# VectorE's two-operand operations read one operand from PSUM, and norms are finished in pairs, in a four-layer graph network on one core

## The chip, the cores and the metric

The kernel runs on one core of one Trainium2 chip. The metric is the device time of the whole program in microseconds (us), the median of three runs. Everything is computed in fp32.

## The reference

Input are 128 graphs of 128 nodes with 512 features each, `x` of 128x128x512, and their adjacency matrices `adj` of 128x128x128, and the weights of four layers. Each layer adds a graph function to `x` and normalises the sum over the features. Cut to what matters here, per graph:

```python
# layer 0: a diffusion with attention weights, three hops
Xw = x @ Wv + bv;  sj, si = Xw @ aw[:512], Xw @ aw[512:]
alpha = adj * exp(leaky_relu(sj[None, :] + si[:, None] + ab, 0.2))
T = alpha / (alpha.sum(-1, keepdims=True) + 1e-12)
H = sum over k in 0..2 of (T^k @ x) @ Wk[k] + bk[k]
x1 = layernorm(x + relu(H))
# layer 1: two hypergraph convolutions, H = (adj != 0)
conv(v, W, b) = Dn * (H @ (Be * (H.T @ (v @ W.T)))) + b
h = layernorm(relu(conv(x1, W1, b1))) * gamma + beta       # 1024 features
x2 = layernorm(x1 + (conv(h, W2, b2) + x1))
# layer 2: s = (x2 @ w) @ a
A = exp(leaky(tanh((s[:, None] + s[None, :]) / 8) * 8, 0.1)) * adj
A = A / A.sum(-1, keepdims=True) * adj.sum(-1, keepdims=True)
x3 = layernorm(x2 + A @ x2 @ w)
# layer 3: attention of 8 heads, scores scaled by 2 * adj, softmax, output product
out = layernorm(x3 + softmax(q k^T / 8 * 2 * adj) v Wo^T + bo)
```

## The kernel before

**Tiling.** One graph is one block of 128 rows. A pair of graphs (`U` = 2) is one tile; a round of `layer0`, `layer1` or `layer23` works on two pairs, so there are 32 rounds of four graphs for each. All of layer 0 is done, then all of layer 1, then layers 2 and 3 together; results pass through DRAM (`x1d`, `x2d`, `x3d`). The large products are split by Strassen's scheme in Winograd's form, seven products of half-size blocks in place of eight (`strassen`, L614), for some weights twice over (`twice`, L817). TensorE gathers into three PSUM banks per scheme; ScalarE copies the first results of a bank out (`plain_take`, L659), VectorE adds the later ones to tiles in SBUF (`biased_take`, L674), and GpSimd makes the sums of the left operands (`lefts`, `operands`).

**The order of the work.** No engine's order is written by hand. Every operation is handed to a planner (`Plan`, L171) with a key (a due time in rounds), and the planner plays all of them through with estimated durations (`estimate`, L122) and hand-off times (`LATENCY`): on each engine it takes the lowest key among those that are ready, gives out buffers as they come free, and at last issues everything in the order of its start times (`emit`, L362). So nearly all instructions have line 373 in the profile, and groups are told apart by tiles. A change of any estimate, tile or dependency can reorder every queue. Engines then run their queues strictly in that order. DMAs are issued on SyncE's queue (SP), save a few at the start.

**What the planner knows of VectorE and GpSimd.** `shares_port` (L148) marks operations that it keeps apart on these two engines: all of GpSimd's but memsets, and of VectorE those with two SBUF operands and one-operand copies and scalar operations from SBUF. In `order` a marked operation starts after the end of the other engine's last marked one (`port`, L284 and L331).

**Buffers.** PSUM has eight banks of 128x512: six named `bank`, and `t0` and `t1`, which layer 0 uses for its hops and which join the banks when layer 0 is over. In SBUF, `four` are tiles of a pair (128x2x512), `sq` pairs of 128x128 matrices, `col` small statistics, `out`, `first`, `side`, `ks` and `rows` large areas that are cut into further `four` tiles when their first use is over. A trace name such as `out<-bank,out` therefore often means a `four` tile that lies in the `out` area.

**The steps that the change touches.**
- Attention terms of layer 0 (L1000 and before) and layer 2 (`layer23`): PE spreads a column over a bank (`spread_pair`, L834); ScalarE applies the nonlinear functions from the bank into an `sq` tile and then within it; VectorE multiplies it by the adjacency matrix, both in SBUF, and sums the rows (`accum_out`); GpSimd divides by the sums, and the matrix goes through DRAM to be turned.
- Counts of layer 1: VectorE takes the maximum of two-column counts with 1.
- Row scale of layer 1: for each graph, VectorE computes `h * dn + b1` over 128x1024 in one operation (`t`, `rows1`), ScalarE applies relu, VectorE takes statistics.
- Norms: `norm_terms` (L690) and `layer_norm` (L701) finish each 128-row block by itself: VectorE sums up the statistics and adds eps, GpSimd raises the variance to the power -1/2, ScalarE multiplies by the mean, ScalarE applies both to the block.
- Closing sum of layer 1: per graph `bw2 * drd + b2` and `2 * x1 + q`, ahead of the last product, then `p * dn + q` from the bank, all on VectorE.
- Layer 3's softmax (`attention`, L1421): the weights go through DRAM to be turned by VectorE, except in the very last pair (`last`), where PE transposes them.

Of the kernel before, what the change touches and what calls it, by code (L numbers as in the profile page):

```python
# [66 lines left out]
SPARE, AHEAD = 4, 6  # L67
SIZE = {"four": U * D, "sq": U * (P + 2), "bank": D, "col": 12, "row": D, "w28": 7168, "q7": 7 * 2 * P,
# [102 lines left out]
class Plan:  # L171
# [64 lines left out]
    def order(self, urgent=None):  # L236
# [71 lines left out]
        while count < n:  # L308
# [21 lines left out]
            if o[6]:  # L330
                port[DVE + POOL - e] = end  # L331
                stale.add(DVE + POOL - e)
# [49 lines left out]
def kernel(  # L382
# [80 lines left out]
    def col(*n):  # L463
        return tile_of("col", *n)
# [225 lines left out]
    def norm_terms(st, n=1):  # L690
        mv = col(2)
        ve.bn_aggr(mv, st[:, :6 * n])
        ve.tensor_scalar(mv[:, 1:2], mv[:, 1:2], EPS, None, op0=OP.add)
        ve.tensor_scalar(mv[:, 0:1], mv[:, 0:1], -1.0, None, op0=OP.mult)
        rstd = col(1)
        po.tensor_tensor(rstd, mv[:, 1:2], neghalf, OP.pow)
        nmr = col(1)
        ac.mul(nmr, mv[:, 0:1], rstd)
        return nmr, rstd

    def layer_norm(t):  # L701

        st = col(12)
        stats(st, 0, t)
        nmr, rstd = norm_terms(st)
        ac.activation(t, t, AF.Identity, bias=nmr, scale=rstd)

    def normed(take, t):

        def then(f, b):  # L710
            def run(p):
                f(p)
                layer_norm(t[:, b])
            return run
        take["c12"] = then(take["c12"], 0)
        take["c21"] = then(take["c21"], 1)
        return take
# [232 lines left out]
    def layer0(i0):  # L950
# [33 lines left out]
        for r, i in enumerate(both):  # L984
            A = load_adj(i)
            plan.key = base + WHENT[0][r]
            s = col(U)
            ac.activation(s, R[r][:, :, 0, 3 * P + 1], AF.Identity, bias=c0)
            pt = spread_pair([R[r][:, b, 0, 3 * P:3 * P + 1].to_broadcast([P, P]) for b in range(U)])
            e = sq()  # L990
            for b in range(U):
                ac.activation(e[:, b], pt[:, b * P:(b + 1) * P], AF.Prelu, bias=s[:, b:b + 1], alpha=0.2)
            ac.activation(e, e, AF.Exp)
            den = col(U)
            for b in range(U):
                ve.scalar_tensor_tensor(e[:, b], e[:, b], 1.0, A[:, b], op0=OP.mult, op1=OP.mult,
                                        accum_out=den[:, b:b + 1])
            ac.activation(den, den, AF.Identity, bias=tiny)
            ve.reciprocal(den, den)
            for b in range(U):  # L1000
                po.tensor_scalar(e[:, b], e[:, b], den[:, b:b + 1], None, op0=OP.mult)
            loads.append(through_dram(e.rearrange("p b (k w) -> p b k w", w=Q), f"e{i}"))
        for r, i in enumerate(both):
            plan.key = base + WHENT[1][r]
            x0 = load_rows(x[i:i + U].rearrange("b p f -> p b f"))
            TT = pair_turned(loads[r])
            for m in (1, 0):
                for b in range(U):
# [5 lines left out]
                    if m:  # L1014
                        ac.copy(to, by)
                    else:
                        ve.scalar_tensor_tensor(x0[:, b], p, 0.0, x0[:, b], op0=OP.max, op1=OP.add)
                        layer_norm(x0[:, b])
# [116 lines left out]
    def layer1(i0):  # L1135
# [5 lines left out]
        for (_, ab), in each(loaded):  # L1141
# [7 lines left out]
            ve.tensor_scalar(cnt, cnt, 1.0, None, op0=OP.max)  # L1149
# [52 lines left out]
        for r, i in enumerate(both):  # L1202
            plan.key = base + STEP1 * (5, 7)[r]
            for b in range(U):
                t = h[r][b].rearrange("p g f -> p (g f)")
                ve.scalar_tensor_tensor(t, t, dns[r][b], rows1[:, :2].rearrange("p g f -> p (g f)"),
                                        op0=OP.mult, op1=OP.add)
                ac.activation(t, t, AF.Relu)
                sts = col(12)
                for g in range(2):  # L1210
                    stats(sts, g, h[r][b][:, g])
                nmr, rstd = norm_terms(sts, 2)
                ac.activation(t, t, AF.Identity, bias=nmr, scale=rstd)
                loads.append(through_dram(h[r][b].rearrange("p (j g) (k w) -> p j (g k) w", j=1, k=2), f"h{i + b}"))
        for r, i in enumerate(both):
# [15 lines left out]
            q = four()  # L1231
            for b in range(U):
                ve.scalar_tensor_tensor(q[:, b], bw2, drds[r][:, b:b + 1], b2_b, op0=OP.mult, op1=OP.add)
                ve.scalar_tensor_tensor(q[:, b], x1[:, b], 2.0, q[:, b], op0=OP.mult, op1=OP.add)
            for b in range(U):
                p = bank()
                pe.matmul(p, K[:, b, :P], G[:, b], start=True, stop=True)
                ve.scalar_tensor_tensor(q[:, b], p, dns[r][b], q[:, b], op0=OP.mult, op1=OP.add)
                layer_norm(q[:, b])
            sp.dma_start(x2d[i // U], q)  # L1240
# [91 lines left out]
    def layer23(i0):  # L1332
# [10 lines left out]
        for i, x2, A in each(both, x2s, As):  # L1343
# [5 lines left out]
            pt = spread_pair([s2[:, b:b + 1].to_broadcast([P, P]) for b in range(U)])  # L1349
            F = sq()  # L1350
            for b in range(U):
                ac.activation(F[:, b], pt[:, b * P:(b + 1) * P], AF.Tanh, bias=s2[:, b:b + 1])
            ac.activation(F, F, AF.Prelu, alpha=0.1)
            ac.activation(F, F, AF.Exp, scale=8.0)
            r = col(U)
            for b in range(U):
                ve.scalar_tensor_tensor(F[:, b], F[:, b], 1.0, A[:, b], op0=OP.mult, op1=OP.mult,
# [63 lines left out]
    def attention(i0, A, qT, kT, v, x3d, base, r):  # L1421
        last = i0 + U == B
# [129 lines left out]
```

## Time and profile before

| | before |
|---|---|
| median of 3 runs (lowest, highest) | 5461.58 us (5458.56, 5464.62) |
| the profiled execution | 5463.22 us, span 5461.4 us |
| mean granted TensorE clock | 0.994 |
| instructions | 93,897 |
| VectorE, attention products sq<-sq,sq 128x128 | 256, 402 ns mean |
| VectorE, row scale 128x1024, in three areas | 63 + 47 + 18, 1619, 1584 and 1722 ns mean |
| VectorE, bank and SBUF, 128x512 (four<-bank,sq) | 72, 679 ns mean |
| GpSimd, powers col<-col,neghalf | 640, 582 ns mean |
| ScalarE, products col<-col,col | 640, 291 ns mean |
| DMA | 815.8 MB, 149 GB/s |

PE is TensorE's matmul row, PEld its weight loads, DVE is VectorE, ACT ScalarE, POOL GpSimd, SP SyncE; `x256` counts records, and an fp32 matmul shows as two. A group line reads: line, engine, operation, tiles written <- tiles read, shape, count, busy us, mean ns, and then the idle time ahead of it with what ended that.

### The profile page before, as it was taken

How to read it: one execution, taken by the hardware profiler on the slowest of the kernel's cores; microseconds unless marked ns; L12 is line 12 of the kernel's file. 1: busy time of each engine (PE TensorE's matmuls, PEld its weight loads, DVE VectorE, ACT ScalarE, POOL GpSimd, SP SyncE). 2: the span in 40 equal slices, each digit the busy share in tenths (PEclk: the TensorE clock that was granted, in tenths of full speed). 3: DMA queues.
4: the chain of work that ended last, by engine and by line, in shares of the span. 5: the costliest groups of instructions: out<-in, count | busy, mean ns of one | idle time of the engine just before them, and what ended most of it. 6: DMA issues, size and time to landing. Idle time of an engine off the chain costs nothing.

```text
span 5461.4 us, 93897 instructions
## 1 busy us (share of the span) xinstructions
PE 5338.6 (98%) x29065; PEld 4256.9 (78%) x29065; DVE 4544.2 (83%) x11573; ACT 2382.0 (44%) x6437; POOL 4032.8 (74%) x4875
## 2 busy tenths in 40 slices
PE   8999999999999999999999999999999999999998
PEld 4555555555778888888888888998999998999987
DVE  6889888887888989998989878787787887787776
ACT  2434433344434444444444344554444444545444
POOL 6777777665777777777777567877777777777776
PEclk9999999999999999999999999999999999999999
DMA  3444444445454554554545645555555555455443
GB/s 100 134 139 125 133 143 128 128 120 162 146 149 150 145 155 150 151 157 147 154 146 150 225 139 159 167 155 157 162 154 164 156 158 161 153 163 162 153 153 123
DMA packets 841933, 815.80 MB, mean 149 GB/s; under 512 B 269388, under 2 KB 640596, under 8 KB 841431
## 3 DMA queue, kind: packets, MB, share of 16 engines
q1 hardware_dynamic: 839926, 807.18, 48.7%
q8 instruction: 230, 3.77, 0.3%
q10 hardware_dynamic: 1504, 2.62, 0.2%
q14 instruction: 273, 2.23, 0.1%
HBM read 459.43 MB, written 350.09 MB: 148 GB/s over the span
## 4 chain that ended last, share of the span: by engine, by line
PE 76%; DVE 10%; DMA 4%; POOL 3%; SPq 3%; issue 2%; ACT 1%; DVEq 0%; POOLq 0%; ACTq 0%
PE bank L373 58%; PE t L373 19%; DVE out L373 3%; DVE four L373 3%; SPq L373 3%; DVE col L373 2%; POOL four L373 1%; DVE side L373 1%; DMA sq<-in_adj_dram 1%; POOL out L373 1%; DMA first<-x3d 1%; DMA four<-in_x_dram 0%; DMA out<-x3d 0%; ACT out L373 0%; DVE sq L373 0%
## 5 line engine op out<-in xcount | busy, mean ns | idle before, releaser
L373 PE MATMUL bank<-first,four 128*128 128x386 f32 (+3 forms) x6114 | 1733.2, 430 | 58.4 <-DVE out L373 21.8
L373 PEld LDWEIGHTS bank<-first,four 128*128 128x128 f32 (+2 forms) x6114 | 1070.3, 189 | 640.1 <-DVE out L373 132.1
L373 DVE TENSOR_TENSOR out<-bank,out 128x386 f32<-128x386 f32 (+1 forms) x2030 | 981.6, 502 | 211.9 <-PE bank L373 164.2
L373 POOL TENSOR_TENSOR col<-col,neghalf 128x1 f32<-128x1 f32 x640 | 368.7, 582 | 452.1 <-DVE col L373 451.5
L373 DVE TENSOR_TENSOR four<-bank,four 128x256 f32<-128x256 f32 x1256 | 514.8, 416 | 177.5 <-PE bank L373 158.3
L373 POOL TENSOR_TENSOR out<-out 128x772 f32<-128x772 f32 (+3 forms) x250 | 350.2, 1408 | 263.2 <-DVE out L373 189.4
L373 PE MATMUL bank<-first,out 128*128 128x256 f32 (+2 forms) x2048 | 498.7, 377 | 7.5 <-DVE side L373 2.8
L373 POOL TENSOR_TENSOR four<-four 128x256 f32<-128x256 f32 (+2 forms) x439 | 357.6, 827 | 142.7 <-DVE four L373 76.1
L373 ACT COPY out<-bank 128x258 f32<-128x258 f32 (+2 forms) x527 | 214.1, 409 | 550.7 <-PE bank L373 414.2
L373 PEld LDWEIGHTS bank<-first,out 128*128 128x128 f32 (+2 forms) x2048 | 372.3, 189 | 77.3 <-issue 9.5
L373 POOL TENSOR_TENSOR four<-four,four 128x256 f32<-128x256 f32 (+2 forms) x479 | 414.0, 869 | 7.2 <-PE bank L373 1.3
L373 ACT ACTIVATE col<-col,col 128x1 f32<-128x1 f32 x640 | 183.9, 291 | 401.0 <-POOL col L373 348.5
L373 PE MATMUL bank<-first 128*128 128x128 f32 (+1 forms) x2356 | 329.6, 278 | 1.9 <-DVE four L373 1.3
L373 ACT ACTIVATE four<-four,col,col 128x512 f32<-128x512 f32 (+1 forms) x367 | 324.2, 887 | 7.4
L373 PEld LDWEIGHTS bank<-first 128*128 128x128 f32 (+1 forms) x2356 | 300.5, 189 | 18.1 <-issue 2.9
L373 PE MATMUL bank<-out,first 128*128 128x128 f32 (+2 forms) x1832 | 301.0, 305 | 1.1 <-DVE col L373 0.8
L373 ACT COPY four<-bank 128x256 f32<-128x256 f32 (+1 forms) x329 | 137.7, 422 | 355.5 <-PE bank L373 333.5
L373 DVE BATCH_NORM_STATS2 col<-four 128x6 f32<-128x512 f32 x430 | 287.6, 678 | 4.8 <-ACT four L373 3.1
L373 PEld LDWEIGHTS bank<-out,first 128*128 128x128 f32 (+1 forms) x1832 | 250.1, 187 | 19.4 <-issue 1.5
L373 PE MATMUL t<-out,sq 128*128 128x512 f32 x512 | 255.5, 594 | 6.4 <-DVE sq L373 2.5
L373 PE MATMUL bank<-four,first 128*128 128x256 f32 (+3 forms) x1424 | 253.3, 322 | 2.7 <-DVE first L373 1.1
L373 ACT COPY t<-out 128x512 f32<-128x512 f32 x256 | 151.0, 591 | 198.6 <-DVE four L373 107.2
(567 smaller groups left out, 12925.7 us busy)
## 6 DMA issues: line engine op xcount, KB each, us to landing
four<-x1d SPq DMA_DIRECT2D x69, 512.0 KB, 5.2
four<-h SPq DMA_DIRECT2D x66, 512.0 KB, 4.5
four<-in_x_dram SPq DMA_DIRECT2D x504, 64.0 KB, 2.1
h<-four SPq DMA_DIRECT2D x252, 128.0 KB, 2.6
four<-in_x_dram SPq DMA_DIRECT2D x60, 512.0 KB, 3.9
x1d<-four SPq DMA_DIRECT2D x60, 512.0 KB, 2.8
four<-S SPq DMA_DIRECT2D x50, 512.0 KB, 4.4
h<-out SPq DMA_DIRECT2D x188, 128.0 KB, 2.4
```

The lines of the kernel that those rows point to most:

```text
L373: call(*map(real, args), **{n: real(a) for n, a in kw.items()})
```

## The change

Six edits, all in how VectorE, ScalarE and GpSimd do the same arithmetic:

1. Attention terms: ScalarE's functions stay in the bank, and VectorE multiplies bank by adjacency matrix into SBUF. The bank is held until then.
2. Layer 1's row scale: ScalarE multiplies each half of `h` by `dn` into a bank, VectorE adds `b1` from SBUF. Two banks and four operations in place of one, per graph.
3. Layer 1's closing sum: after the product, `p * dn + b2` and `bw2 * drd + p` are written back to the bank, then `2 * x1 + p` into `x1`; the tile `q` is gone.
4. Norms: the terms of a pair's two blocks are finished together, one GpSimd power and one GpSimd product of two columns each; the product was ScalarE's.
5. Counts: the two-column maximum becomes two one-column ones.
6. The planner leaves 20 ns on VectorE's side after a GpSimd operation (`YIELD`); and the path without DRAM in `attention` is taken by the last two pairs, not the last one.

```diff
@@ -65,6 +65,7 @@
 QW = 3 * P + 2
 SLACK = 60
 SPARE, AHEAD = 4, 6
+YIELD = 20
 SIZE = {"four": U * D, "sq": U * (P + 2), "bank": D, "col": 12, "row": D, "w28": 7168, "q7": 7 * 2 * P,
         "w7": 7 * QW, "out": U * 4 * QW, "t0": D, "t1": D, "row1": 4 * D, "k": U * (P + 2),
         "prep": U * D}
@@ -328,7 +329,7 @@
                 reached = o[8]
                 stale.add(SP)
             if o[6]:
-                port[DVE + POOL - e] = end
+                port[DVE + POOL - e] = end + (YIELD if e == POOL else 0)
                 stale.add(DVE + POOL - e)
             count += 1
             for tile in o[5]:
@@ -687,30 +688,39 @@
     def stats(st, k, piece):
         ve.bn_stats(st[:, 6 * k:6 * k + 6], piece)
 
-    def norm_terms(st, n=1):
-        mv = col(2)
-        ve.bn_aggr(mv, st[:, :6 * n])
-        ve.tensor_scalar(mv[:, 1:2], mv[:, 1:2], EPS, None, op0=OP.add)
-        ve.tensor_scalar(mv[:, 0:1], mv[:, 0:1], -1.0, None, op0=OP.mult)
-        rstd = col(1)
-        po.tensor_tensor(rstd, mv[:, 1:2], neghalf, OP.pow)
-        nmr = col(1)
-        ac.mul(nmr, mv[:, 0:1], rstd)
-        return nmr, rstd
-
-    def layer_norm(t):
-
-        st = col(12)
-        stats(st, 0, t)
-        nmr, rstd = norm_terms(st)
-        ac.activation(t, t, AF.Identity, bias=nmr, scale=rstd)
+    def norm_terms(sts):
+
+        mv = col(2 * U)
+        for b, st in enumerate(sts):
+            ve.bn_aggr(mv[:, 2 * b:2 * b + 2], st)
+            ve.tensor_scalar(mv[:, 2 * b + 1:2 * b + 2], mv[:, 2 * b + 1:2 * b + 2], EPS, None, op0=OP.add)
+            ve.tensor_scalar(mv[:, 2 * b:2 * b + 1], mv[:, 2 * b:2 * b + 1], -1.0, None, op0=OP.mult)
+        mean, var = (mv.rearrange("p (b k) -> p k b", k=2)[:, k] for k in range(2))
+        rstd = col(U)
+        po.tensor_tensor(rstd, var, neghalf.to_broadcast([P, U]), OP.pow)
+        nmr = col(U)
+        po.tensor_tensor(nmr, mean, rstd, OP.mult)
+        return [(nmr[:, b:b + 1], rstd[:, b:b + 1]) for b in range(U)]
+
+    def layer_norms():
+
+        sts = []
+
+        def one_more(t):
+            sts.append((t, col(6)))
+            stats(sts[-1][1], 0, t)
+            if len(sts) == U:
+                for (t, _), (nmr, rstd) in zip(sts, norm_terms([st for _, st in sts])):
+                    ac.activation(t, t, AF.Identity, bias=nmr, scale=rstd)
+        return one_more
 
     def normed(take, t):
+        norm = layer_norms()
 
         def then(f, b):
             def run(p):
                 f(p)
-                layer_norm(t[:, b])
+                norm(t[:, b])
             return run
         take["c12"] = then(take["c12"], 0)
         take["c21"] = then(take["c21"], 1)
@@ -987,13 +997,13 @@
             s = col(U)
             ac.activation(s, R[r][:, :, 0, 3 * P + 1], AF.Identity, bias=c0)
             pt = spread_pair([R[r][:, b, 0, 3 * P:3 * P + 1].to_broadcast([P, P]) for b in range(U)])
+            for b in range(U):
+                ac.activation(pt[:, b * P:(b + 1) * P], pt[:, b * P:(b + 1) * P], AF.Prelu, bias=s[:, b:b + 1], alpha=0.2)
+            ac.activation(pt[:, :U * P], pt[:, :U * P], AF.Exp)
             e = sq()
-            for b in range(U):
-                ac.activation(e[:, b], pt[:, b * P:(b + 1) * P], AF.Prelu, bias=s[:, b:b + 1], alpha=0.2)
-            ac.activation(e, e, AF.Exp)
             den = col(U)
             for b in range(U):
-                ve.scalar_tensor_tensor(e[:, b], e[:, b], 1.0, A[:, b], op0=OP.mult, op1=OP.mult,
+                ve.scalar_tensor_tensor(e[:, b], pt[:, b * P:(b + 1) * P], 1.0, A[:, b], op0=OP.mult, op1=OP.mult,
                                         accum_out=den[:, b:b + 1])
             ac.activation(den, den, AF.Identity, bias=tiny)
             ve.reciprocal(den, den)
@@ -1004,6 +1014,7 @@
             plan.key = base + WHENT[1][r]
             x0 = load_rows(x[i:i + U].rearrange("b p f -> p b f"))
             TT = pair_turned(loads[r])
+            norm = layer_norms()
             for m in (1, 0):
                 for b in range(U):
                     p = tile_of(("t0", "t1")[b], D)
@@ -1015,7 +1026,7 @@
                         ac.copy(to, by)
                     else:
                         ve.scalar_tensor_tensor(x0[:, b], p, 0.0, x0[:, b], op0=OP.max, op1=OP.add)
-                        layer_norm(x0[:, b])
+                        norm(x0[:, b])
                 plan.key += .2
             sp.dma_start(x1d[i // U], x0)
 
@@ -1146,7 +1157,8 @@
             for b in range(U):
                 ve.tensor_scalar(HT[:, b], AT[:, b], 0.0, None, op0=OP.not_equal, op1=OP.add,
                                         accum_out=cnt[:, b:b + 1])
-            ve.tensor_scalar(cnt, cnt, 1.0, None, op0=OP.max)
+            for b in range(U):
+                ve.tensor_scalar(cnt[:, b:b + 1], cnt[:, b:b + 1], 1.0, None, op0=OP.max)
             ve.reciprocal(cnt, cnt)
             HB = sq(M)
             for b in range(U):
@@ -1201,15 +1213,19 @@
         loads = []
         for r, i in enumerate(both):
             plan.key = base + STEP1 * (5, 7)[r]
-            for b in range(U):
+            sts = []
+            for b in range(U):
+                sts.append(col(12))
+                for g in range(2):
+                    p = bank()
+                    ac.mul(p, h[r][b][:, g], dns[r][b])
+                    ve.tensor_tensor(h[r][b][:, g], p, rows1[:, g], OP.add)
                 t = h[r][b].rearrange("p g f -> p (g f)")
-                ve.scalar_tensor_tensor(t, t, dns[r][b], rows1[:, :2].rearrange("p g f -> p (g f)"),
-                                        op0=OP.mult, op1=OP.add)
                 ac.activation(t, t, AF.Relu)
-                sts = col(12)
                 for g in range(2):
-                    stats(sts, g, h[r][b][:, g])
-                nmr, rstd = norm_terms(sts, 2)
+                    stats(sts[b], g, h[r][b][:, g])
+            for b, (nmr, rstd) in enumerate(norm_terms(sts)):
+                t = h[r][b].rearrange("p g f -> p (g f)")
                 ac.activation(t, t, AF.Identity, bias=nmr, scale=rstd)
                 loads.append(through_dram(h[r][b].rearrange("p (j g) (k w) -> p j (g k) w", j=1, k=2), f"h{i + b}"))
         for r, i in enumerate(both):
@@ -1228,16 +1244,15 @@
             K = tile_of("k", U, M)
             sp.dma_start(K.rearrange("p b n -> p (b n)"), kept[r], run=U * M)
 
-            q = four()
-            for b in range(U):
-                ve.scalar_tensor_tensor(q[:, b], bw2, drds[r][:, b:b + 1], b2_b, op0=OP.mult, op1=OP.add)
-                ve.scalar_tensor_tensor(q[:, b], x1[:, b], 2.0, q[:, b], op0=OP.mult, op1=OP.add)
+            norm = layer_norms()
             for b in range(U):
                 p = bank()
                 pe.matmul(p, K[:, b, :P], G[:, b], start=True, stop=True)
-                ve.scalar_tensor_tensor(q[:, b], p, dns[r][b], q[:, b], op0=OP.mult, op1=OP.add)
-                layer_norm(q[:, b])
-            sp.dma_start(x2d[i // U], q)
+                ve.scalar_tensor_tensor(p, p, dns[r][b], b2_b, op0=OP.mult, op1=OP.add)
+                ve.scalar_tensor_tensor(p, bw2, drds[r][:, b:b + 1], p, op0=OP.mult, op1=OP.add)
+                ve.scalar_tensor_tensor(x1[:, b], x1[:, b], 2.0, p, op0=OP.mult, op1=OP.add)
+                norm(x1[:, b])
+            sp.dma_start(x2d[i // U], x1)
 
 
     h = D // 2
@@ -1347,14 +1362,14 @@
             deg = col(U)
             ve.tensor_reduce(deg, A, AX.X, OP.add)
             pt = spread_pair([s2[:, b:b + 1].to_broadcast([P, P]) for b in range(U)])
+            for b in range(U):
+                ac.activation(pt[:, b * P:(b + 1) * P], pt[:, b * P:(b + 1) * P], AF.Tanh, bias=s2[:, b:b + 1])
+            ac.activation(pt[:, :U * P], pt[:, :U * P], AF.Prelu, alpha=0.1)
+            ac.activation(pt[:, :U * P], pt[:, :U * P], AF.Exp, scale=8.0)
             F = sq()
-            for b in range(U):
-                ac.activation(F[:, b], pt[:, b * P:(b + 1) * P], AF.Tanh, bias=s2[:, b:b + 1])
-            ac.activation(F, F, AF.Prelu, alpha=0.1)
-            ac.activation(F, F, AF.Exp, scale=8.0)
             r = col(U)
             for b in range(U):
-                ve.scalar_tensor_tensor(F[:, b], F[:, b], 1.0, A[:, b], op0=OP.mult, op1=OP.mult,
+                ve.scalar_tensor_tensor(F[:, b], pt[:, b * P:(b + 1) * P], 1.0, A[:, b], op0=OP.mult, op1=OP.mult,
                                         accum_out=r[:, b:b + 1])
             ve.reciprocal(r, r)
             for b in range(U):
@@ -1419,7 +1434,7 @@
             attention(i, As[r], *qk[r], vs[r], x3ds[r], base, r)
 
     def attention(i0, A, qT, kT, v, x3d, base, r):
-        last = i0 + U == B
+        last = i0 + 2 * U >= B
         plan.key = base + WHENS[r]
         loads, PTs = [], []
         Ns = [four() for _ in range(U if last else 0)]
```

## The prediction, before the changed kernel ran

> **What bounds the kernel now.** I read the page's busy shares first, then the chain that ended last, then the busy time of each engine by stage.
>
> ```profile
> PE 5338.6 (98%) x29065; PEld 4256.9 (78%) x29065; DVE 4544.2 (83%) x11573; ACT 2382.0 (44%) x6437; POOL 4032.8 (74%) x4875
> ...
> PE 76%; DVE 10%; DMA 4%; POOL 3%; SPq 3%; issue 2%; ACT 1%; DVEq 0%; POOLq 0%; ACTq 0%
> ```
>
> By stage the columns are: stretch in us from the span's start, its length, busy us of PE, PE's weight loads, VectorE (DVE), ScalarE (ACT) and GpSimd (POOL), each with its count, the granted clock, the DMA share, GB/s.
>
> ```profile
> 0.00:60.00 60.00, 39.15 (x112) 22.80 (x113) 32.43 (x51) 9.07 (x23) 28.99 (x34) 0.77 0.56 138
> 60.00:1300.00 1240.00, 1215.81 (x3631) 657.29 (x3630) 1057.51 (x2632) 495.84 (x1160) 890.27 (x1038) 1.00 0.43 126
> 1300.00:1800.00 500.00, 472.52 (x2142) 375.00 (x2141) 433.11 (x1081) 203.26 (x384) 356.57 (x439) 0.99 0.52 157
> 1800.00:3000.00 1200.00, 1190.72 (x5708) 1013.18 (x5707) 1078.21 (x2735) 503.00 (x931) 906.48 (x1109) 1.00 0.51 151
> 3000.00:3300.00 300.00, 288.04 (x1680) 249.72 (x1679) 238.60 (x594) 122.34 (x330) 191.31 (x229) 1.00 0.57 180
> 3300.00:5300.00 2000.00, 1990.95 (x14748) 1812.45 (x14747) 1593.17 (x4215) 972.63 (x3353) 1550.54 (x1904) 1.00 0.52 159
> 5300.00:5461.40 161.40, 141.44 (x1053) 126.43 (x1051) 111.21 (x271) 75.85 (x258) 108.59 (x125) 0.95 0.38 124
> ```
>
> TensorE is the limit. Its idle time is all that the change can win: stage length minus PE busy gives 20.9, 24.2, 27.5, 9.3, 12.0, 9.1 and 20.0 us, 123 together, 2.2% of the span. Start-up and end hold 41 of it; the change touches the end a little and the start not at all. Layers 2 and 3 (3300 to 5300) have 9 us in 2000, so nothing done to VectorE there can pay. The prize lies in layer 0, the hand-over to layer 1 and the hand-over to layer 2: 24 + 28 + 12.
>
> Who makes PE late there? The waits of PE, and the timelines of VectorE, GpSimd and PE around the worst stall:
>
> ```profile
> PE bank L373 <- DVE out L373: 25.6, 27, 3.4
> PE bank L373 <- DVE four L373: 17.9, 19, 4.2
> ```
> ```profile
> 1480.50 4.91 DVE L373 SCALAR_TENSOR_TENSOR four<-four,col,rows 128x1024 f32<-128x1024 f32 x1
> 1485.34 0.41 DVE L373 TENSOR_TENSOR side<-bank,side 128x256 f32<-128x256 f32 x1
> 1485.78 4.44 DVE L373 SCALAR_TENSOR_TENSOR side<-side,col,rows 128x1024 f32<-128x1024 f32 x1
> ...
> 1491.53 1.93 PE L373 MATMUL bank<-first,four 128*128 128x256 f32 x6 [4.19 <-DVE four L373]
> ```
> ```profile
> L373 DVE SCALAR_TENSOR_TENSOR sq<-sq,sq x256: 242/286/2084, 64.8 to 5315.2; 128x128 f32<-128x128 f32 x128
> ...
> L373 POOL TENSOR_TENSOR col<-col,neghalf x640: 537/549/1586, 102.5 to 5456.0; 128x1 f32<-128x1 f32 x160
> ```
>
> The two row scales of layer 1, at best 1.23 us each, take 4.9 and 4.4 us while GpSimd runs one operation after another; the PSUM evacuation queued behind them is late and PE stands 4.19 us. The last two lines are min/median/max in ns: an operation with two SBUF operands is stretched up to eightfold, and GpSimd's power threefold when it loses.
>
> [...]the form with one PSUM operand (out<-bank,row, 128 columns, 256 of them) runs 245 to 294 ns, never more. [...]680 ns (four<-bank,sq, 128x512) against 683 (four<-four,four), medians. [...]a bank kept for ScalarE and VectorE work is lost to PE meanwhile; that is the price side here. [...]256-column records shown as 0.38 us start every 0.216 us, so I also counted lateness from start to start.
>
> **The change, part by part.**
>
> VectorE work. (a) Attention terms: 256 at 402 ns mean become 256 at 286 (median; the PSUM form's 285 agrees; ends 242 and 294): -30 us. (b) Row scale: 128 with 207 us together (means 1584 to 1722) become 256 additions of 128x512 from a bank at 680: 174 us, -33. Unhindered it is 1.36 us against 1.27, so this gain is all lock. (c) Closing sum: 127 + 104 + 95 = 326 us (bias and product 992 mean, 2*x1 815, final 741) become 128 x (741 + 741 + 680) = 277: -49. VectorE writing PSUM is not in the trace; 741 is the same form into SBUF[...]. (d) The 64 two-column maxima (mean 339, max 1228) become 128 one-column ones at 142: -3. (e) Two 128x1024 transposes fewer: -2. Sum -117 of 4544.
>
> ScalarE: 640 products at 291 ns go (-186); 256 scalings SBUF to PSUM come. Not in the trace: a 128x512 copy to PSUM is 590, a scale and bias pair adds 183 at 1024 columns (1241 against 1058), so 590 + 92 = 682, ends 590 and 814: +175. In-place PSUM attention steps: within 10 us either way. Four more copies of 1.07. At 44% busy this hides, but for its order: a scaling waits for the last VectorE or GpSimd piece of h, and behind it in ScalarE's queue stand the copies out of the Strassen banks, for which PE waits.
>
> GpSimd: 640 powers (373 us) become 320 of two columns and 320 products of two columns (196 median for col<-col,ks). A two-column power isn't shown: 549 if the width is free, 1098 if it doubles; I take 600: 192 + 63 = 255, -118 (ends -134 and +42). More: GpSimd waits 452 us at the powers for VectorE's variance, with the Strassen operand sums queued behind; that happens half as often.
>
> Pairs: the first row block of a pair waits for the second, about 1.4 us in layer 0 and 4 to 5 us in layer 1, and its four h stores on SP, with SP loads behind them, go that much later. The work lies stages ahead in steady state; only at the hand-overs I charge 2 us (0 to 6).
>
> Banks: a layer 1 scale holds one for 0.68 + 0.68 + two hand-offs of about 0.2 + queueing, some 2 to 4 us; 8 of them per round of four items (32 rounds in about 54 us each) use 16 to 32 of 8 x 54 = 432 bank us, and the closing banks live 1.4 us longer, 6 more: 5 to 9%. I charge 4 us (0 to 45).
>
> End: the second last pair also goes through PE transposes: two stores, two loads (4.4 us median to landing) and the VectorE transposes leave its path; 16 transposes at 0.22 us = 3.5 us of PE. PE stands 6.33 us there, waiting for GpSimd's softmax scale, and in the changed program's PE order these transposes and that pair's Strassen product stand among the last pair's. -5 net (-8 to -1). Very last: both normalisations in a row (+0.81) for one ScalarE product less: +0.6. The planner's 20 ns pause is only in its model.
>
> Now PE. From start to start, I counted lateness over 0.13 us, and what of it ended within 4 us after a changed operation that was stretched by over 0.3 us: 8.9 of 34.5 us in layer 0 (such moments are 4% of the time, so 1.4 by chance), 13.1 of 35.6 from 1300 to 1800 (31%: 11 by chance, but the two largest, 4.4 and 3.6 us, stand against operations of 4.4 and 4.5 us), 0.5 of 13.7 to 3000, 6.0 of 15.5 to 3300 (2.6 by chance), 0 after. So 28 at most; beyond chance 7.5 + 8 + 3.4 = 19. I take -19. From VectorE's queue being shorter altogether I take -5 (0 to 20), from fewer power waits on GpSimd -2 (0 to 6).
>
> Sum: -19 - 5 - 2 - 5 + 0.6 + 4 + 2 = -24.4 against the profiled execution's 5463.2 us (span 5461.4 and 1.8 around it): 5438.8. The median of the runs is 1.6 lower: **5437 us**. What is late next: the same evacuations in their own order, and ScalarE's copies.
>
> **Rivals.** *VectorE's relief spreads:* with evacuations on time PE loses half of its 73 us of mid-run idle, 36 and not 19 + 5 + 2, and the end gives 8 with ScalarE's price near nought: about -50, 5411. For it: weight loads wait 147 us for "DVE out", mostly hidden. Against: much mid-run lateness has no stretched operation before it. *Nothing to tell:* PE's idle only changes its cause, since an order written anew for 94,000 instructions has its own stalls; 5460. For it: 120 us saved lie beside a PE at 98%. *Slower:* layer 1's banks. PE runs there at 99.2%, VectorE at 90%; if each of 128 row blocks' scale and closing makes PE wait 0.19 us, the 24 us are gone; at 0.35 us it is 45 more than none, 5482. For it: ScalarE's queue joins a path where PE waits at once. Against: ScalarE is 42% busy there and the bank share is below 10%. *That the operands don't move* is excluded: the built program shows 256 attention products reading banks.
>
> **Chances.** Forecast 0.52 (5416 to 5450 by its terms' ends), spread relief 0.20 (5390 to 5416), nothing 0.13, slower 0.15. About 0.2%, 11 us, is what a measurement of this kernel can tell from no change. Faster 0.72, same 0.13, slower 0.15. From 5395 to 5474 some 0.05 is left below and 0.14 above.
>
> **What would show it.** Attention products at 286 ns and never above 300; the row additions at 680; no VectorE operation over 3 us in layer 1; powers at about 600. PE idle from 60 to 1300 near 15 us, to 1800 near 17. Wrong: PE waits on ScalarE or for banks in layer 1 above 20 us, or VectorE shrinking by 117 us with PE's idle unchanged.

## The result, and the profile after

The changed kernel takes 5422.74 us (median of 4 runs, 5420.25 to 5423.49) against 5462.50 (5458.56 to 5464.62) for the kernel before, taken beside it: 39.8 us less, a ratio of 0.9927 with a 95% interval of 0.991 to 0.9944. Its profiled execution has a span of 5420.9 us at a granted clock of 0.997, against 5461.4 at 0.994. That is faster, within the 5416 to 5450 us of the forecast, and by 15 us more than the 24.4 it had as its point.

The first two lines that the prediction showed, from the page of the kernel after:

```profile
PE 5326.9 (98%) x29081; PEld 4246.0 (78%) x29081; DVE 4448.5 (82%) x11763; ACT 2374.5 (44%) x6057; POOL 3877.5 (72%) x4875
...
PE 86%; DVE 5%; DMA 3%; issue 2%; POOL 2%; ACT 1%; SPq 1%; DVEq 0%; ACTq 0%; POOLq 0%
```

VectorE loses 95.7 us and GpSimd 155.3. In the chain of work that ended last VectorE falls from 10% to 5%, TensorE rises from 76% to 86%: the end is now set nearly everywhere by TensorE's own work. The stages, with the columns that the prediction explains:

```profile
0.00:60.00 60.00, 35.45 (x96) 21.29 (x96) 28.57 (x42) 8.30 (x19) 31.91 (x46) 0.92 0.55 127
60.00:1300.00 1240.00, 1218.78 (x3639) 658.47 (x3640) 1045.10 (x2639) 472.75 (x1046) 866.54 (x1025) 1.00 0.43 126
1300.00:1800.00 500.00, 486.19 (x2252) 393.85 (x2251) 420.50 (x1201) 231.71 (x401) 335.36 (x470) 0.99 0.54 168
1800.00:3000.00 1200.00, 1194.62 (x5757) 1016.36 (x5756) 1036.01 (x2859) 564.57 (x936) 815.05 (x1106) 1.00 0.50 151
3000.00:3300.00 300.00, 294.67 (x1809) 257.82 (x1808) 238.03 (x634) 124.33 (x336) 195.79 (x250) 1.00 0.59 189
3300.00:5300.00 2000.00, 1990.08 (x14726) 1804.70 (x14725) 1601.31 (x4196) 915.71 (x3131) 1557.32 (x1896) 1.00 0.52 158
5300.00:5420.90 120.90, 107.06 (x811) 93.47 (x810) 78.99 (x197) 57.11 (x188) 75.53 (x86) 0.98 0.32 105
```

Stage length minus PE busy is now 24.6, 21.2, 13.8, 5.4, 5.3, 9.9 and 13.8 us. The hand-over into layer 1 (27.5 before), the end of layer 1 (12.0) and the end of the program (20.0) gave most (the last stretch is now 40 us shorter, so it holds less work than the one before); layers 2 and 3 gave nothing; the first 60 us got worse (96 matmul records against 112 by then). Idle time falls by 29 us in all and PE's busy time by 11.7, though it has no less to do. A matmul's record is longer than its turn (256 columns in the kernel after: 0.379 us from its start to its end, 0.216 from one start to the next, medians), so I count from start to start below.

TensorE's waits, and the tiles that the prediction showed (min/median/max ns):

```profile
PE bank L374 <- DVE out L374: 21.7, 33, 2.5
PE bank L374 <- DVE first L374: 20.4, 7, 10.8
PE bank L374 <- DVE four L374: 9.3, 16, 2.4
```
```profile
L374 DVE SCALAR_TENSOR_TENSOR sq<-bank,sq x212: 251/286/297, 70.7 to 5278.0; 128x128 f32<-128x128 f32 x106
...
L374 DVE TENSOR_TENSOR four<-bank,rows x115: 424/681/693, 1377.2 to 5190.8; 128x512 f32<-128x512 f32 x111, 128x256 f32<-128x256 f32 x4
...
L374 POOL TENSOR_TENSOR col<-col,neghalf x320: 690/706/1211, 101.9 to 5414.5; 128x2 f32<-128x2 f32 x160
```

The products' longest is 297 ns where it was 2084, and no row addition is above 694 ns where a row scale took 4909. The waits for "DVE out" and "DVE four" lose 12.5 us. The line "DVE first" stands at 20.4, half of it one stall of 10.8 us at the start (53 to 64 us), where the kernel before stands 3.8.

For what follows I use the prediction's count: TensorE's lateness from one matmul's start to the next, over 0.13 us, in us by stage; the runs of the lower rows are explained below. Stages of different kernels shift a little, so a row is read for its large figures; `locks_lay1` ends 170 us later than the others, so its later columns hold earlier work.

| kernel | 0 to 90 | to 1290, layer 0 | to 1500 | to 1800 | to 2950, layer 1 | to 3100 | to 3300 | to 5200, layers 2, 3 | end |
|---|---|---|---|---|---|---|---|---|---|
| before | 30.2 | 28.8 | 24.3 | 11.5 | 12.8 | 5.0 | 11.4 | 11.6 | 16.1 |
| after | 34.3 | 23.2 | 15.1 | 3.7 | 7.3 | 4.0 | 4.2 | 11.1 | 10.7 |
| layer1_only | 28.7 | 29.9 | 18.5 | 0.2 | 0.0 | 5.2 | 15.8 | 14.2 | 16.6 |
| no_pairs | 35.2 | 24.8 | 19.9 | 0.0 | 0.0 | 6.4 | 10.6 | 13.1 | 12.3 |
| yield0 | 28.5 | 20.4 | 16.3 | 3.7 | 6.7 | 1.8 | 6.8 | 36.5 | 10.9 |
| no_locks_scalars | 33.8 | 28.6 | 17.4 | 1.9 | 5.0 | 5.0 | 5.2 | 8.9 | 10.8 |
| locks_att | 35.7 | 33.4 | 17.8 | 2.1 | 5.4 | 4.6 | 4.9 | 8.4 | 10.5 |
| locks_lay1 | 35.2 | 24.5 | 23.1 | 24.3 | 96.8 | 12.8 | 17.0 | 19.7 | 12 |
| last_old | 34.0 | 25.9 | 16.6 | 2.6 | 7.8 | 3.9 | 3.1 | 12.5 | 16.8 |

Before sums to 151.7 and after to 113.6: 38.1 less, nearly all of the 40.5 us between the two spans. Delays under 0.13 us are not in the table. Added up from the traces, the control `no_locks_scalars` has 8 us more of them than the changed kernel and `no_pairs` 8 us fewer, so a row's sum follows the time to some 8 us at best.

### The profile page after: what moved, and what is told of

Read it like the earlier page. It is cut to its first block, busy times and chain, and to the rows that moved or that the text cites. A ratio compares the mean times of both kernels' runs of the same rounds, so it can differ in the third digit from the quotient of the medians.

```text
span 5420.9 us, 93833 instructions
## 1 busy us (share of the span) xinstructions
PE 5326.9 (98%) x29081; PEld 4246.0 (78%) x29081; DVE 4448.5 (82%) x11763; ACT 2374.5 (44%) x6057; POOL 3877.5 (72%) x4875
## 4 chain that ended last, share of the span: by engine, by line
PE 86%; DVE 5%; DMA 3%; issue 2%; POOL 2%; ACT 1%; SPq 1%; DVEq 0%; ACTq 0%; POOLq 0%
PE bank L374 65%; PE t L374 21%; DVE out L374 2%; DVE four L374 1%; DVE col L374 1%; DMA four<-in_x_dram 1%; SPq L374 1%; POOL four L374 1%; ACT out L374 0%; DVE first L374 0%; POOL out L374 0%; POOL first L374 0%; DMA sq<-in_adj_dram 0%; DMA out<-x3d 0%; DVE side L374 0%
## 5 line engine op out<-in xcount | busy, mean ns | idle before, releaser
L374 POOL TENSOR_TENSOR col<-col,neghalf 128x2 f32<-128x2 f32 x320 | 234.4, 732 | 375.4 <-DVE col L374 373.3
L374 PE MATMUL bank<-first,out 128*128 128x256 f32 (+1 forms) x1912 | 458.1, 374 | 10.5 <-DVE four L374 5.1
L374 PEld LDWEIGHTS bank<-first,out 128*128 128x128 f32 (+1 forms) x1912 | 340.0, 187 | 77.7 <-DVE four L374 12.6
L374 PE MATMUL bank<-four,first 128*128 128x256 f32 (+3 forms) x1832 | 321.9, 320 | 2.4 <-ACT first L374 0.9
L374 ACT ACTIVATE four<-four,col,col 128x512 f32<-128x512 f32 (+1 forms) x282 | 253.3, 923 | 131.5 <-POOL col L374 126.5
L374 PEld LDWEIGHTS bank<-four,first 128*128 128x128 f32 (+2 forms) x1832 | 253.8, 182 | 33.2 <-DVE first L374 3.2
L374 PE MATMUL bank<-out,first 128*128 128x128 f32 (+2 forms) x1636 | 269.4, 300 | 2.0 <-DVE out L374 1.6
L374 ACT ACTIVATE out<-out,col,col 128x512 f32<-128x512 f32 (+1 forms) x191 | 166.9, 903 | 192.8 <-POOL col L374 192.7
L374 DVE TENSOR_TENSOR four<-t,four 128x256 f32<-128x256 f32 x434 | 181.4, 419 | 82.9 <-PE t L374 74.8
L374 DVE BATCH_NORM_STATS2 col<-four 128x6 f32<-128x512 f32 x356 | 236.5, 681 | 4.0 <-ACT four L374 1.7
```

Source lines behind the costliest of these rows:

```text
L374: call(*map(real, args), **{n: real(a) for n, a in kw.items()})
```

## The experiments

Theory: VectorE's operations with two SBUF operands stand behind GpSimd's, and what queues behind them on VectorE makes TensorE late; the change removes those operations. Rivals: the gain comes from norms in pairs; or from nothing but a new order of 94,000 instructions. In this part "lock" stands for what the theory supposes, that one of the two engines stands while the other works; in a trace it would be a stretched operation, as the products of 242 to 2084 ns in the kernel before.

**sbuf_operands.** The changed kernel, its split operations and pairs kept, but results put into SBUF first:

```diff
-                    p = bank()
-                    ac.mul(p, h[r][b][:, g], dns[r][b])
-                    ve.tensor_tensor(h[r][b][:, g], p, rows1[:, g], OP.add)
+                    ac.mul(h[r][b][:, g], h[r][b][:, g], dns[r][b])
+                    ve.tensor_tensor(h[r][b][:, g], h[r][b][:, g], rows1[:, g], OP.add)
```

The closing sum (through a tile `q`) and the attention products likewise.

> The changed kernel with its operations as they are, in number and split, but with both operands of the attention products, of layer 1's row-scale additions and of two of the three closing additions in SBUF again; norms in pairs and the end path stay. Theory of the lock (VectorE's two-SBUF operations stand behind GpSimd's): about 5450 us (5440 to 5462), row-scale additions of 680 ns unhindered at over 850 ns mean, attention products near 400. Rival, pairs (fewer GpSimd powers and no ScalarE products make the gain): at most 5430. Rival, a luckier order whatever the operations: anything, but no stretched operations ahead of PE's stalls.

Measured: 5544.66 us, ratio 1.0147 (1.0129 to 1.0164): 122 above the changed kernel. The direction is the lock's, the size is far above the expected range. TensorE was 57.3 us late in layer 1's steady stretch, against 7.3. The plan differs too, so this run alone doesn't separate the two.

**layer1_only.** The kernel before, with the row scale and closing sum of layer 1 read from banks (edits 2 and 3 of the change), nothing else.

> The kernel before with only layer 1's row scale and closing sum changed to read from banks. Lock: most of the gain, since lateness of PE between 1290 and 3300 us fell by 31 of 40 us: 5432 us (5425 to 5440). Pairs: 5455 or more. Banks as a cost: above 5455 with PE's waits in layer 1 up.

Measured: 5437.03 us, ratio 0.9948 (0.9931 to 0.9964): 25 to 29 below the kernel before. In the table, 1290 to 3300 falls from 65.0 to 39.7, and layer 1 between 1500 and 2950 has next to none (0.2). Layer 0, which this run leaves alone, is as late as before (29.9 against 28.8). These two edits are the larger part of the result, as far as a newly planned run can tell (see yield0).

**no_pairs.** The changed kernel with each block's norm finished by itself, as before.

> The changed kernel with each block's norm finished by itself again (640 one-column powers on GpSimd, 640 products on ScalarE). Lock: 5427 us (5421 to 5434), pairs being worth a few us. Pairs: 5440 or more.

Measured: 5423.8 us, ratio 0.9924 (0.9906 to 0.9942): the same as the changed kernel. ScalarE has its 640 products back (2575.9 us busy against 2374.5) and nothing is lost by it. Pairs are worth nothing in total. The table shows 11 us more lateness with them in layer 1 and some 20 less around it; most of the 9 us between the sums is made up by delays under 0.13 us.

**yield0.** `YIELD = 0` in place of 20: the same operations, planned with 20 ns less.

> The changed kernel with the planner's pause of 20 ns after GpSimd's operations set to nought, so that all orders are planned anew with the same operations. Lock and pairs both: 5423 us within 6. If orders by themselves are worth tens of us: off by more than 10.

Measured: 5437.94 us, ratio 0.9953 (0.9935 to 0.9971). A miss. The same operations in another order are 15 us slower, with 25 us more lateness in layers 2 and 3, where the change does next to nothing, and less elsewhere. So an experiment that is planned anew can be off by that much for its order alone, and the next ones keep the plan.

**locks_all, and its control no_locks_scalars.** The planner is handed the changed kernel's operands (`like`), so that all five engines get the changed kernel's instructions in the same order; only what VectorE reads differs. (The traces of both kernels and of the changed one, spans of 5603.4, 5431.8 and 5420.9 us, show one and the same order on TensorE, VectorE, ScalarE and GpSimd.) A bank's first column as per-partition factor keeps each operation waiting for the same producer:

```diff
-                    ve.tensor_tensor(h[r][b][:, g], p, rows1[:, g], OP.add)
+                    ve.scalar_tensor_tensor(h[r][b][:, g], h[r][b][:, g], p[:, :1], rows1[:, g], like=(p, rows1), op0=OP.mult, op1=OP.add)
```

The same for the attention products and two closing operations. The control has the factor but reads the bank, `p, p[:, :1], rows1[:, g]`.

> The changed kernel with its plan kept instruction for instruction on all five engines (the planner is shown the operands of the changed kernel), but 256 attention products, 256 row-scale additions and two of three closing operations on 128 blocks read both large operands from SBUF; a bank's first column stands in as the per-partition factor, so that each waits for the same as before. This leaves out the attention coefficients, the row scale and part of the closing sum: values change, work and order don't. Lock theory: in sbuf_operands products took 348 ns against 286, row additions 908 against 681, closing operations some 230 more each, so VectorE gets some 130 us longer and TensorE stalls grow in layer 1 as they did there: 5480 (5450 to 5550). Re-planning theory (the 122 us of sbuf_operands came from its other order): below 5440.

> The control of locks_all: the same plan and the same per-partition factors from a bank, but the large operand read from the bank as in the changed kernel. It leaves the same parts of the computation wrong-valued. The factor adds some 60 ns to 640 VectorE operations, 38 us beside other work. Lock theory: 5427 (5420 to 5436), so that nearly the whole of locks_all's loss is the lock. If the longer operations themselves are what costs: as slow as locks_all.

Measured: 5608.87 us (5605.36 to 5613.66), ratio 1.0278 (1.026 to 1.0295), and for the control 5434.4 (5433.54 to 5435.11), 0.9955 (0.994 to 0.997). The same instructions in the same order differ by 174 us for their operand's place. That is the lock, and above the expected range of 5450 to 5550, which was scaled from sbuf_operands, where the planner could still keep the two engines apart. A rival is that an operation on two SBUF operands is slower by itself. It isn't: the shortest of the 256 row additions takes 707 ns in locks_all and 715 in the control, while the means are 1132 and 745. 11.7 us over the changed kernel is the price of some 60 ns more in each of 640 operations of the control (products 285 to 349 ns, row additions 681 to 744, in the means of their largest groups).

**locks_att and locks_lay1.** The two parts of locks_all, each alone.

> The part of locks_all in the two attentions alone: the 256 products of layers 0 and 2 read both operands from SBUF, in the changed kernel's plan (attention coefficients left out of the values). In locks_all the products took 440 ns against 349 in its control, 23 us of VectorE, and outside layer 1 TensorE was some 20 us later than in the control. If that is theirs: 5446 (5436 to 5458). If the loss outside layer 1 was only layer 1's carried along: 5430 or less.

> The other part of locks_all: row-scale additions and two of three closing operations of layer 1 with both operands in SBUF, in the changed kernel's plan (row scale and part of the closing sum left out of the values). By the stages of locks_all (TensorE 97 us late in layer 1's steady stretch against 5, and 40 more around it): 5580 (5555 to 5600). If the locks of attention and of layer 1 only hurt together: below 5540.

Measured: 5439.56 us (5438.17 to 5440.53) and 5591.15 (5588.08 to 5595.15). Against the changed kernel that is +17 and +168, together the 186 of locks_all: the parts add. Of the 17 the control explains 12 or fewer, so locks on short products cost 5 us or somewhat more; those on the 512-column operations of layer 1 cost 156 to 168. Their lines, groups by shape (busy us, mean ns, idle before with its releaser), first locks_lay1, then the control. Groups go by tiles, so the first one of locks_lay1 holds 43 closing operations beside the 111 row additions that the control's first one has:

```profile
L374 DVE SCALAR_TENSOR_TENSOR four<-four,bank,rows 128x512 f32<-128x512 f32 x154 | 168.3, 1095 | 11.4 <-ACT bank L374 11.4
L374 DVE SCALAR_TENSOR_TENSOR bank<-rows,col 128x512 f32<-128x512 f32 x94 | 100.8, 1073 | 0.4
L374 DVE SCALAR_TENSOR_TENSOR bank<-bank,col,rows 128x512 f32<-128x512 f32 x94 | 70.3, 749 | 4.4 <-PE bank L374 4.4
```
```profile
L374 DVE SCALAR_TENSOR_TENSOR four<-bank,rows 128x512 f32<-128x512 f32 x111 | 82.4, 744 | 10.2 <-ACT bank L374 9.8
L374 DVE SCALAR_TENSOR_TENSOR bank<-bank,col,rows 128x512 f32<-128x512 f32 x94 | 70.6, 752 | 4.4 <-PE bank L374 4.3
L374 DVE SCALAR_TENSOR_TENSOR bank<-rows,col,bank 128x512 f32<-128x512 f32 x94 | 70.2, 748 | 0.4
```

The comparison stands within locks_lay1 itself: `bank<-bank,col,rows` has one large SBUF operand and takes 749 ns, as in the control; `bank<-rows,col`, the same operation on two of them, takes 1073. How that reaches TensorE shows in the timelines of VectorE, GpSimd and TensorE in locks_lay1 (start us, length us, engine and operation, and in brackets the idle time before with its releaser):

```profile
1944.58 1.80 DVE L374 SCALAR_TENSOR_TENSOR four<-four,bank,rows 128x512 f32<-128x512 f32 x1
1946.30 1.22 DVE L374 SCALAR_TENSOR_TENSOR bank<-rows,col 128x512 f32<-128x512 f32 x1
1947.43 0.41 DVE L374 TENSOR_TENSOR four<-t,four 128x256 f32<-128x256 f32 x1
...
1944.54 1.29 POOL L374 TENSOR_TENSOR four<-side,four 128x512 f32<-128x512 f32 x1
1945.78 1.18 POOL L374 TENSOR_TENSOR side<-four,side 128x256 f32<-128x256 f32 x1
1946.92 1.74 POOL L374 TENSOR_TENSOR four<-side,out 128x512 f32<-128x512 f32 x1
...
1947.99 0.67 PE L374 MATMUL t<-first,side 128*128 128x256 f32 x2 [1.41 <-DVE four L374]
```

VectorE's addition begins 0.04 us after a GpSimd operation and ends only 0.55 us after that one's end at 1945.83; the next ends 0.56 us after GpSimd's next one, at 1946.96. Then GpSimd itself takes 1.74 us for what took 1.29. The small evacuation at 1947.43, which reads one operand from PSUM, is not stretched itself (0.41 us; the 434 of its form take 417 ns in the mean) but comes some 1.5 us late (1.80 and 1.22 us where two unhindered ones take about 0.75 each), and TensorE stands 1.41 us for it. In this stretch the operation that began second was the stretched one, VectorE's of 1.80 and 1.22 us and GpSimd's of 1.74, and what was queued behind it was late with it; that it is so every time was not shown.

From 1800 to 3000, locks_lay1 first and the control second, TensorE is behind by 73 us of busy time and 511 records, while VectorE is busier (1071 us against 1049) with less work done (2629 records against 2873):

```profile
1800.00:3000.00 1200.00, 1123.24 (x5239) 918.56 (x5240) 1071.46 (x2629) 516.62 (x855) 850.85 (x1014) 1.00 0.46 139
```
```profile
1800.00:3000.00 1200.00, 1196.29 (x5750) 1015.20 (x5749) 1049.48 (x2873) 562.01 (x935) 818.39 (x1111) 1.00 0.50 151
```

**att_old.** The changed kernel with both attentions as before, planned anew.

> The changed kernel with both attentions as before (exponentials in SBUF, products of two SBUF operands), planned anew with the lock known to the planner. Lock theory: the planner avoids part of the 20 us that the same locks cost unplanned, so slower by 3 to 20: 5432 (5422 to 5445). If the attention part of the change is worth nothing: 5417 to 5424.

Measured: 5446.19 us (5440.88 to 5451.6), ratio 0.9969 (0.9958 to 0.9981): 23 above the changed kernel, a little over the expected range. 12 of the 23 lie in layers 2 and 3 (TensorE 23.0 us late there against 11.1), where the same locks cost nothing in the changed kernel's plan (locks_att 8.4, control 8.9). So about half of this run's loss looks like plan, not lock; the rest is 11 us or so.

**last_old.** `last = i0 + U == B`, as before; the plan is unchanged up to the last stretch.

> The changed kernel with the round trip through DRAM kept for the attention of the last pair but one, as before; nothing ahead of the last stretch is changed. The prediction put 5 us on this edit; the stretch from 5200 us on was 16.1 us late before and 10.7 after: 5428 (5425 to 5431). If that gain was luck of the plan: 5423.

Measured: 5427.12 us (5424.34 to 5430.59), ratio 0.9934 (0.9919 to 0.9948): 4.4 above the changed kernel, and the end of the program is 16.8 us late against 10.7. This edit is worth the 5 us put on it.

**pairs_not_hidden and hybrid_start.** Attempts at a better version: norms in pairs but for layer 1's hidden activations; and with that, the start's copies all on ScalarE:

```diff
-            for b, (nmr, rstd) in enumerate(norm_terms(sts)):
+            for b in range(U):
+                (nmr, rstd), = norm_terms(sts[b:b + 1])
...
-                (ac.copy, ve.tensor_copy)[g](W[j]
+                ac.copy(W[j]
```

> The changed kernel with the hidden activations of layer 1 normed block by block, all other norms in pairs. By the stages of no_pairs, pairs cost TensorE 11 us in layer 1's steady stretch (7.3 and 3.7 us late against 0) and win as much elsewhere. If that is the pairs' delay: 5412 (5406 to 5419). If it is the luck of a new plan, as yield0 was: anywhere from 5412 to 5440.

> pairs_not_hidden, and the copies that lay out layer 0's operands in the first 90 us all on ScalarE, none on VectorE (a VectorE copy with both sides in SBUF stands behind GpSimd, and TensorE waits 10.8 us for one at 53 us). If the start's stall goes and nothing takes its place: 8 us below pairs_not_hidden, 5404 (5396 to 5412). If ScalarE becomes late instead: level with it or above.

Measured: 5417.62 us (5416.64 to 5431.21), ratio 0.993 (0.9915 to 0.9945), and 5418.4 (5416.59 to 5423.29), ratio 0.9927 (0.9912 to 0.9942). That is 6 and 14 us above what was hoped for; the first lies at the upper end of its range, the second outside its own. The intervals are the changed kernel's own, so no version is shown to beat it. In the first, layer 1's lateness from 1500 to 2950 is 6.1 us against 11.0, not 0 as in no_pairs: the hidden norm is half of the pairs' cost there at most. In the second the stall of 10.8 us is gone, but stalls of 7.3 and 3.4 us stand in its place, and the first 90 us have 30.8 us of lateness against 34.3. The expectation misread that stall: TensorE waited there for a VectorE sum that itself waited for GpSimd's sums (below), not for a copy. The copies do lose time, but less: 0.42 us alone, 0.83 to 1.09 us beside GpSimd's sums.

## Why the prediction was right, and where its sizes were off

**What bounds the kernel.** Right: TensorE's lateness is all that was won. The prize lay in the hand-overs as said, less in layer 0 (5.6 us of lateness gone; PE idle 21.2 us where near 15 was expected) than in the 65 us from 1290 to 3300 (30.7 gone; PE idle to 1800 is 13.8 where near 17 was expected). "Nothing done to VectorE there can pay" held for layers 2 and 3: 11.6 to 11.1.

**VectorE's work.** Predicted -117, measured -95.7. The terms that were worked out came: (a) 256 products, 102.8 us to 73.0, -30 as predicted; (b) row scale 207.4 to 174.6, -33 as predicted; (c) closing sum -47 against -49, since the two operations that write a bank take 747 and 757 ns and not 741; (d) counts nothing against -3. What was missed is an operation that the change doesn't touch: the 128 scores of layer 2 (`junk<-...,row`), still with two SBUF operands, went from 711 to 912 ns in the mean, 26 us. So operations that the change leaves alone were stretched more in the new order. These terms are sums of durations. All of VectorE's durations added up fall by 69.7 us; its busy time falls by more because records that overlap count once in it (the one at 1946.30 us in locks_lay1 begins 0.08 us before the end of the one ahead), so the terms don't add up to the 95.7.

**ScalarE.** -7.5 us, predicted -11; the scaling into a bank takes 690 ns against the 682 that were estimated, and TensorE waited for ScalarE in layer 1 just once, for 0.6 us. The slower rival's mechanism, banks and ScalarE's queue, didn't appear: layer1_only has those banks and no stall in layer 1 from 1500 to 2950. The 4 us charged for it look too many.

**GpSimd.** The power was the mis-sized price: 600 ns for two columns was taken, the trace has 706 (median, 732 mean), so powers and products save 74 us and not 118. The waits at the powers didn't halve: 451.8 us to 385.5. That GpSimd still shrank by 155 is in good part the lock's other side: 589 sums of 512 columns with two tiles take 1302 ns in the mean, where 583 took 1351, and sums of 256 columns 748 and 742 against 762 and 759, with medians level within 2 ns. The powers' part moved nothing at TensorE: no_pairs is as fast.

**Lateness taken from TensorE.** This is the step that was off in size. The terms "locks -19", "queue -5", "power waits -2", banks +4 and pairs +2 made -20 between start and end; the table gives -36.8 from 90 to 5200. The count put a TensorE stall down to the lock only if it ended within 4 us after a stretched operation, and found 0.5 of 13.7 us in layer 1's steady stretch. Its 8 us for 1300 to 1800 were not an excess over chance either (13.1 counted, 11 by chance), but two stalls picked by their size. Yet layer1_only, which removes layer 1's locks, empties that stretch and the one before it (24.3 us to 0.2) and takes 25 us in all where the count had 11 for layer 1 and its borders. My reading is that locks delay a queue that is 90% busy, and the delay reaches TensorE later, through an operation that is itself not stretched, as at 1947 us in locks_lay1; how long such a delay lives was not measured. The rival "VectorE's relief spreads" had this mechanism and 36 us for it; its parts make 44 and not the 50 that it gave, and its 5411 lies 12 us below the measured time, the forecast's 5437 lies 14 above: between the two sizes the result doesn't decide.

**End and start.** -4.4 predicted for the end, -5.4 in the table, 4.4 by last_old. The start got 4.1 us worse, which had no term: GpSimd now makes four first-layer sums together at 57.15 us, VectorE's next sum waits 8.81 us for them and TensorE 10.81. None of these operations is in the diff; so I put it down to the new plan.

Sum: -36.8 - 5.4 + 4.1 = -38.1, where -24.4 stood. Is the surplus luck? The planner's pause of 20 ns, which the prediction left unpriced as "only in its model", reorders every queue: without it the same operations take 5437.9 us (yield0), by chance the forecast itself. But in layers 0 and 1, from 90 to 3300 us, all three plans with the operands moved have the gain: 93.8 us of lateness before, 57.5 in the changed kernel, 55.7 in yield0, 61.7 in no_pairs. yield0 loses its 15 us in layers 2 and 3. So some 32 to 38 us in layers 0 and 1 are not one plan's luck, while the total can't be told to better than some 15 us. The 174 us between locks_all and its control are what locks cost in a plan that doesn't know of them; the kernel before had a plan made to keep them apart, and paid some 25 for them in layer 1 by layer1_only. The shares of the result are thus estimates: layer 1 about 25, the end 4, attention between 5 (locks_att less the control's factor) and 23 (att_old), pairs nothing.

## What to carry to other kernels

Beside a busy GpSimd, a VectorE operation with two SBUF operands cost here not only its own stretching (1073 ns against 749 with one of them in PSUM, 128x512, in locks_lay1) but a delay of what was queued behind it (1.5 us at 1947 us): put one operand in PSUM first where the operation is long and its queue feeds TensorE (156 to 168 us here), and leave the short ones for later (some 5 us). To price one cause in a kernel whose order is planned, keep the plan and change only the operand; a run that is planned anew has an error of its own, here 15 us. An operation count that falls (320 powers, 640 ScalarE products) was worth nothing here, where TensorE hardly waited for those engines. And a setting that only reorders the plan, like the 20 ns pause, belongs among the edits to be tested alone.

## What the runs showed of the hardware

- Both engines were stretched: in locks_all GpSimd's 512-column sums with two tiles took 1357 ns in the mean against 1302 in the control, and VectorE's 256 row additions 1132 against 745.
- A power of two columns on GpSimd takes 706 ns against 549 for one, medians; if that is linear, an estimate from these two, 392 fixed and 157 for each column.
- A VectorE operation that reads one operand from a bank and writes a bank takes 747 to 757 ns in the mean in the changed kernel, where the form from bank to SBUF takes 741 in the kernel before (128x512 with a per-partition factor).
- The six VectorE copies from SBUF to SBUF at the changed kernel's start (`first<-first`, 128x512, 25 to 47 us) take 415 and 418 ns with GpSimd idle, and 829 to 1090 ns while GpSimd adds tiles.
- Lengthening 640 VectorE operations by some 60 ns without any lock (31.4 us of VectorE's busy time, the control) cost 11.7 us: with VectorE 82% busy, over a third of its added time came through to the end.
